# Two elementwise steps of a mixture-of-experts combine moved from VectorE to GpSimd, with other buffer counts

## The chip, the cores and the metric

The kernel runs on one core of a Trainium2 chip. The core has five instruction queues that run side by side and meet through semaphores: TensorE (PE in the profile; its weight loads are PEld), VectorE (DVE), ScalarE (ACT), GpSimd (POOL) and SyncE (SP, which here only starts transfers). Every queue works in the order of its program: an instruction that waits holds back all that stand behind it on its engine. The metric is the device time of one execution in microseconds (us).

## The reference

One transformer block over x of shape (4, 2048, 256), with shifts, scales and gates that come from a conditioning vector:

```python
h = _layernorm(x, axis=-1) * (1 + ca) + sa
x = x + ga * _L0_attn_ref(h, ...)            # 8 heads, causal, a geometric term in the scores
h = _layernorm(x, axis=-1) * (1 + cb) + sb
x = x + gb * _L0_ffn_ref(h, ...)             # 2 shared experts + 16 routed, 4 for each token

# inside _L0_ffn_ref
probs = jax.nn.softmax(xt @ router_w.T, axis=-1)
topk_p, topk_i = jax.lax.top_k(probs, TOP_K)
act = jax.nn.gelu(up_r, approximate=False) * gate[:, :, None]
routed = jnp.einsum('tre,rhe->th', act, routed_down)
return (shared + routed).reshape(b, s, h)
```

All arrays are 32-bit floats. For the part that is changed this is what counts: a token's result is its row after attention and shared experts, plus gb times the weighted sum of four routed experts' outputs.

## The kernel before

The 8192 tokens are worked on in 16 blocks of 512 (`QB`), each in four tiles of 128 (`P`). A loop over the blocks (line 1440) alternates two stages. In a fill-in stage (`fill_in`) TensorE does projections, the output product, the shared experts and tiles of routed experts, mixed with the searches for the score maxima (ps on TensorE, parts on VectorE). In an attention stage (`sum_steps`) it computes scores (st), the products with the values (av) and the sums of the probabilities (dv); VectorE adds neighbouring probability tiles (p<-p,p) so that some dv products can be left out.

The blocks 0 to 13 send their tokens to experts in five groups of 2 or 3 blocks. For a group, GpSimd scatters the tokens' rows into a DRAM table xg, ordered by expert (`scatter`). `tile_steps` fetches tiles of that table (xr) and the weights of their experts (wt) by SyncE, turns them (px), multiplies (pu, py) and writes the outputs to a table yg. Blocks 14 and 15 run all experts densely at the end (`dense_steps`; the weighting of the experts is act<-pw,act on VectorE and the output products are pd).

`combine_steps` (line 1227) brings a group's outputs back. There are 14 x 4 = 56 tiles. For each tile there are:

- `gather`, four times: GpSimd fetches one expert's rows for the 128 tokens from yg by an indirect transfer into got. With the first, SyncE loads row, the tokens' rows after attention and shared experts, from the DRAM tensor pre.
- `combine`: first the stores that are due are issued on SyncE. Then VectorE adds up the four rows with their weights into acc (named sum in the profile), in one TENSOR_SCALAR and three SCALAR_TENSOR_TENSOR instructions.
- `complete`: acc is multiplied by gbs (the gate gb) and row is added. The store to the output is put on a list and issued by the next tile's `combine`.

The order on every engine is the order in which the Python code issues the instructions (`Pinned`, line 43). What sets it here is `tick` (line 501), called at planned moments. A tick first does the next step of a `combine`/`complete` pair that is due, and then one scatter or one gather. A pair falls due three ticks after the last gather of its tile, so in a steady run the order on the queues is: gather 0, 1 and 2 of tile t+1, where `combine` of tile t comes with gather 2; then `complete` of t; then gather 3 of t+1. A new tile's gathers start only while fewer than two pairs are outstanding. Every gather also waits for the last ScalarE instruction issued before it (`paced`). In fill-in stages inside the loop ticks issue gathers but no pairs; pairs wait for the attention stage. After the loop, pairs are issued in all stages.

got, row and sum come from the pool `work`, which keeps two buffers of each unless told otherwise. A load into a buffer waits until the readers of its earlier content are done; so does a computation that writes into one, and a store counts as a reader until its transfer has ended.

Of the kernel before, what the change touches and what calls it, by code (L numbers as in the profile page):

```python
# [12 lines left out]
F32 = mybir.dt.float32  # L13
AF = mybir.ActivationFunctionType
ALU = mybir.AluOpType
# [4 lines left out]
P = 128  # L20
# [74 lines left out]
def adaln_block_kernel(  # L95
# [13 lines left out]
    nc = Engines(tc)  # L109
    B, T, C = x.shape  # L110
# [9 lines left out]
    NB = T // QB  # L120
# [17 lines left out]
    of = out.flatten_outer_dims()  # L138
# [6 lines left out]
    work = ctx.enter_context(tc.tile_pool(name="work", bufs=2))  # L145
# [53 lines left out]
    for k in range(KC):  # L199
# [11 lines left out]
        out=kmask,  # L211
        in_=kmask,
# [43 lines left out]
    for pc in pieces:  # L256
# [6 lines left out]
        out=earlier,  # L263
        in_=earlier,
# [57 lines left out]
    gbs = const.tile([P, B, C], F32, tag="gbs", name="gbs")  # L322
# [173 lines left out]
    stores = []  # L496

    def paced(made):
        nc.gpsimd.behind(made, nc.scalar.last, mybir.DependencyClass.Sync)
# [60 lines left out]
    with tc.tile_pool(name="setup", bufs=1) as setup:  # L560
        wm = setup.tile([P, KC, 6 * C], F32, tag="wm", name="wm")
        nc.scalar.dma_start(
            out=wm[:, :, : 2 * C], in_=wmod[:, : 2 * C].rearrange("(k p) n -> p k n", p=P)
        )
        nc.scalar.dma_start(
            out=wm[:, :, 2 * C :], in_=wmod[:, 2 * C :].rearrange("(k p) n -> p k n", p=P)
# [660 lines left out]
    def combine_steps(group):  # L1227

        n = group.n

        def gather(j, t, k, held):
            i = group.blocks[j]
            at = i * QB + t * P
            if k == 0:
                held["got"] = work.tile([P, TOPK, C], F32, tag="got", name=f"got{i}_{t}")
                held["row"] = work.tile([P, C], F32, tag="row", name=f"row{i}_{t}")
                nc.sync.dma_start(out=held["row"], in_=pre[at : at + P])
            paced(
                nc.gpsimd.indirect_dma_start(
                    out=held["got"][:, k, :],  # L1240
                    out_offset=None,
                    in_=yg[n % 2][: group.nt * P],
                    in_offset=bass.IndirectOffsetOnAxis(
                        ap=group.at[:, j * TT + t, k : k + 1], axis=0
                    ),
                )
            )

        def combine(j, t, held):
            i = group.blocks[j]  # L1250
            got = held["got"]
            while stores:
                stores.pop(0)()
            acc = work.tile([P, C], F32, tag="sum", name=f"sum{i}_{t}")
            held["acc"] = acc
            weight = group.weight[:, j * TT + t]
            nc.vector.tensor_scalar(acc, got[:, 0, :], weight[:, 0:1], None, ALU.mult)
            for k in range(1, TOPK):
                nc.vector.scalar_tensor_tensor(
                    acc, got[:, k, :], weight[:, k : k + 1], acc, ALU.mult, ALU.add  # L1260
                )

        def complete(j, t, held):
            i = group.blocks[j]
            at = i * QB + t * P
            acc, row = held["acc"], held["row"]
            nc.vector.tensor_tensor(acc, acc, gbs[:, i // NB, :], ALU.mult)
            nc.vector.tensor_tensor(acc, acc, row, ALU.add)
            stores.append(lambda: nc.sync.dma_start(out=of[at : at + P], in_=acc))

        out = []
        for j in range(len(group.blocks)):
            for t in range(TT):
                held = {}
                out.append(
                    (
                        [partial(gather, j, t, k, held) for k in range(TOPK)],
                        [partial(combine, j, t, held), partial(complete, j, t, held)],
                    )
                )  # L1280
        return out
# [158 lines left out]
    for i in range(NBLK):  # L1440
# [4 lines left out]
        if i:  # L1445
# [21 lines left out]
            at = max(6, len(mid) - len(finals))  # L1467
# [41 lines left out]
        for n, (_, ss, turn) in enumerate(rest):  # L1509
            at = int(0.93 * (n + 0.5) / len(rest) * ks)  # L1510
# [93 lines left out]
    for e in range(0, R, 4):  # L1604
        nc.sync.dma_start(
            out=resident[:, e * 2 * C : (e + 4) * 2 * C].rearrange("p (e n) -> p e n", e=4),
            in_=experts[e : e + 4].rearrange("e p n -> p e n"),
# [10 lines left out]
    i, j = DENSE  # L1618
# [75 lines left out]
```

## Time and profile before

| | |
|---|---|
| median of 3 runs | 2449.56 us (2446.26 to 2451.17) |
| the profiled execution's own time | 2462.32 us |
| its span, first to last instruction | 2460.6 us |
| mean granted TensorE clock | 0.971 |
| sum<-got,weight on VectorE (56) | 347 ns median |
| sum<-got,weight,sum on VectorE (168) | 485 ns median |
| got<-yg,at on GpSimd (224) | 949 ns median |
| VectorE's waits for a landing of out<-sum | 31.5 us, 8 times, longest 8.4 |
| SyncE's waits put down to VectorE's sum | 308.6 us, 34 times, longest 61.3 |

A name such as sum<-got,weight is a group of instructions that write the tile sum and read got and weight. In groups the columns are shape, count, busy us and mean ns of one, and idle us of the engine just before, with what ended it. In timelines they are start, duration, engine, line, operation, names, shapes and count, and in brackets the idle time before with its releaser. Most instructions pass through one helper, so their line is L54 and the names tell them apart. The profiled execution took 12.8 us longer than the median run.

### The profile page before, as it was taken

The page shows a single profiled execution, that of the slowest core. Times are in us where ns is not written, and L with a number is a line of the kernel's source. Part 1 is how long each engine was busy: PE and PEld are TensorE (multiplying, and loading weights), DVE is VectorE, ACT ScalarE, POOL GpSimd, SP SyncE. Part 2 cuts the span into 40 slices and gives each one's busy share as a digit, 9 for nine tenths or more (in the row PEclk, how much of TensorE's full clock was granted, in tenths as well). Part 3 has the DMA queues.
Part 4 walks back from the last instruction along what each step waited for, and adds up shares of the span by engine and source line. Part 5 has one row for each costly group of instructions (what it writes and reads, how often), then busy time and mean ns, then how long its engine had stood idle before and what let it go on. Part 6 is the DMA issues. An engine that isn't in the chain of part 4 may idle for free.

```text
span 2460.6 us, 42133 instructions
## 1 busy us (share of the span) xinstructions
PE 2318.8 (94%) x16625; PEld 1150.2 (47%) x16625; DVE 1439.9 (59%) x2789; ACT 981.6 (40%) x1391; POOL 732.5 (30%) x740
## 2 busy tenths in 40 slices
PE   7999999999999999999999998998899998998998
PEld 4443434345554334354645435354555634436765
DVE  5676664536674775646674656857564675634325
ACT  2223243543334334533343344643344345552421
POOL 3201010331101244601013342511344125466325
PEclk9889999999999999998999999999999999999999
DMA  3200401343440223323533326222654754427964
GB/s 122 91 1 10 154 10 49 117 162 129 127 155 10 65 65 97 100 86 109 181 120 127 116 63 200 68 89 95 210 188 160 256 161 122 146 72 271 361 202 122
DMA packets 219702, 306.88 MB, mean 125 GB/s; under 512 B 18544, under 2 KB 158832, under 8 KB 219504
## 3 DMA queue, kind: packets, MB, share of 16 engines
q1 hardware_dynamic: 192720, 228.89, 28.5%
q0 software_dynamic: 25536, 73.43, 9.2%
q8 instruction: 131, 2.15, 0.4%
q10 hardware_dynamic: 1248, 1.86, 0.2%
q14 instruction: 67, 0.55, 0.1%
HBM read 193.49 MB, written 114.82 MB: 125 GB/s over the span
## 4 chain that ended last, share of the span: by engine, by line
PE 83%; DVE 6%; ACT 3%; issue 3%; DMA 2%; POOL 1%; another core or an unknown queue 1%; SPq 0%; ACTq 0%; DVEq 0%; POOLq 0%
PE st L54 17%; PE ps L54 13%; PE av L54 11%; PE dv L54 8%; PE pu L54 8%; PE py L54 6%; DVE parts L54 3%; PE pv L54 3%; PE ppq L54 2%; PE px L54 2%; PE po L54 2%; PE pd_s L54 2%; PE pd L54 2%; PE ppk L54 2%; PE pl L54 1%
## 5 line engine op out<-in xcount | busy, mean ns | idle before, releaser
L54 DVE TENSOR_REDUCE parts<-ps 128x2 f32<-128x1024 f32 (+3 forms) x640 | 662.6, 1063 | 323.9 <-PE ps L54 309.7
L54 ACT ACTIVATE p<-st 128x1024 f32<-128x1024 f32 (+3 forms) x640 | 539.3, 894 | 522.9 <-PE st L54 424.2
L54 PE MATMUL st<-qT,kv 32*128 32x512 f32 (+3 forms) x2560 | 404.2, 579 | 16.2 <-ACT p L54 9.8
L54 PE MATMUL ps<-kv,qT 32*128 32x512 f32 (+3 forms) x2560 | 381.9, 602 | 15.6 <-DVE parts L54 10.3
L54 POOL DMA_INDIRECT got<-yg,at x224 | 228.4, 1020 | 332.1 <-ACT p L54 97.6
L54 PE MATMUL av<-p,kv 128*32 128x512 f32 (+3 forms) x2560 | 307.1, 547 | 4.3 <-ACT p L54 3.1
L74 POOL DMA_INDIRECT xg<-rows,at x219 | 219.6, 1003 | 254.0 <-ACT p L54 93.9
L54 PEld LDWEIGHTS st<-qT,kv 32*128 32x128 f32 x2560 | 143.6, 184 | 269.8 <-issue 144.2
L54 PE MATMUL dv<-p,ones 128*32 128x512 f32 (+3 forms) x2224 | 254.0, 527 | 2.2 <-issue 1.9
L54 DVE TENSOR_TENSOR ps<-ps,cmask 128x256 f32<-128x256 f32 x256 | 109.3, 427 | 215.9 <-PE ps L54 184.7
L54 PEld LDWEIGHTS ps<-kv,qT 32*128 32x128 f32 x2560 | 124.2, 190 | 194.1 <-issue 95.2
L54 POOL TENSOR_TENSOR x<-x,tmps 128x512 f32<-128x512 f32 x28 | 35.4, 1265 | 481.3 <-DVE tmps L54 481.2
L54 PE MATMUL py<-wt,tact 128*128 128x256 f32 x608 | 162.2, 401 | 4.7 <-ACT xt L54 2.2
L54 PE MATMUL st<-mT,unit 3*128 3x512 bf16 (+3 forms) x1280 | 165.0, 347 | 0.0
L54 PEld LDWEIGHTS pu<-xt,wt 128*128 128x128 f32 x1216 | 147.6, 194 | 36.5 <-issue 19.8
L54 PE MATMUL pu<-xt,wt 128*128 128x128 f32 x1216 | 158.6, 282 | 3.6 <-DMA wt<-experts 2.5
L54 ACT COPY y<-py 128x512 f32<-128x512 f32 x152 | 89.1, 586 | 164.0 <-PE py L54 160.6
L54 PEld LDWEIGHTS py<-wt,tact 128*128 128x128 f32 x608 | 110.0, 194 | 58.6 <-ACT xt L54 15.0
L54 DVE TENSOR_TENSOR p<-p,p 128x1024 f32<-128x1024 f32 x84 | 106.4, 1307 | 37.9 <-PE av L54 36.8
L54 PEld LDWEIGHTS dv<-p,ones 128*32 128x32 f32 x2224 | 63.3, 110 | 137.4 <-issue 125.7
L54 ACT COPY xt<-px 128x512 f32<-128x512 f32 x152 | 86.6, 587 | 91.4 <-PE px L54 88.8
L54 POOL TENSOR_TENSOR xnb<-xnb,gm 128x256 f32<-128x256 f32 x128 | 106.6, 840 | 47.7 <-issue 19.7
(290 smaller groups left out, 2416.4 us busy)
## 6 DMA issues: line engine op xcount, KB each, us to landing
wt<-experts SPq DMA_DIRECT2D x304, 256.0 KB
xr<-xg SPq DMA_DIRECT2D x76, 512.0 KB
yg<-y SPq DMA_DIRECT2D x76, 512.0 KB
xg<-zeros SPq DMA_DIRECT2D x16, 1024.0 KB
xin<-in_x SPq DMA_DIRECT2D x16, 512.0 KB
x<-in_x SPq DMA_DIRECT2D x16, 512.0 KB
h2d<-xnb POOLq DMA_DIRECT2D x14, 512.0 KB
pre<-x POOLq DMA_DIRECT2D x14, 512.0 KB
```

The costliest lines, as they stand in the source:

```text
L54: made = call(*args, **kwargs)
L74: made = call()
```

## The change

The two instructions of `complete` are issued on GpSimd in place of VectorE. The second one writes its result into row instead of acc, and the output is stored from row. row gets three buffers in place of two and sum one in place of two, so the memory taken is the same.

```diff
-                held["row"] = work.tile([P, C], F32, tag="row", name=f"row{i}_{t}")
+                held["row"] = work.tile([P, C], F32, bufs=3, tag="row", name=f"row{i}_{t}")
...
-            acc = work.tile([P, C], F32, tag="sum", name=f"sum{i}_{t}")
+            acc = work.tile([P, C], F32, bufs=1, tag="sum", name=f"sum{i}_{t}")
...
             acc, row = held["acc"], held["row"]
-            nc.vector.tensor_tensor(acc, acc, gbs[:, i // NB, :], ALU.mult)
-            nc.vector.tensor_tensor(acc, acc, row, ALU.add)
-            stores.append(lambda: nc.sync.dma_start(out=of[at : at + P], in_=acc))
+            nc.gpsimd.tensor_tensor(acc, acc, gbs[:, i // NB, :], ALU.mult)
+            nc.gpsimd.tensor_tensor(row, row, acc, ALU.add)
+            stores.append(lambda: nc.sync.dma_start(out=of[at : at + P], in_=row))
```

## The prediction

> **What bounds the kernel now.** I read the page's busy shares and its chain first, to see which engine sets the end:
>
> ```profile
> span 2460.6 us, 42133 instructions
> ...
> PE 2318.8 (94%) x16625; PEld 1150.2 (47%) x16625; DVE 1439.9 (59%) x2789; ACT 981.6 (40%) x1391; POOL 732.5 (30%) x740
> ...
> PE 83%; DVE 6%; ACT 3%; issue 3%; DMA 2%; POOL 1%; another core or an unknown queue 1%; SPq 0%; ACTq 0%; DVEq 0%; POOLq 0%
> ```
>
> TensorE is the bound nearly everywhere. A saving on VectorE counts only where TensorE stood still for it. So the question is which of the 56 combined tiles sit at such a spot, and what GpSimd's queue does with the steps it gets. Second, the groups by shape, VectorE then GpSimd, for the two steps that move and for the nearest row on their new engine (the same shape, two SBUF operands):
>
> ```profile
> L54 DVE TENSOR_TENSOR sum<-sum,row 128x256 f32<-128x256 f32 x56 | 26.5, 473 | 1.9
> L54 DVE TENSOR_TENSOR sum<-sum,gbs 128x256 f32<-128x256 f32 x56 | 25.2, 450 | 0.9
> ```
>
> ```profile
> L54 POOL TENSOR_TENSOR xnb<-xnb,gm 128x256 f32<-128x256 f32 x128 | 106.6, 840 | 47.7 <-issue 19.7 <-DVE xnb L54 16.9 <-PE st L54 5.5
> ```
>
> Third, the views by tile, for the spread (min/median/max in ns):
>
> ```profile
> L54 POOL TENSOR_TENSOR xnb<-xnb,gm x128: 721/736/1763, 215.4 to 2256.2; 128x256 f32<-128x256 f32 x128
> ```
>
> ```profile
> L54 DVE TENSOR_TENSOR p<-p,p x84: 1206/1219/2185, 478.9 to 2194.3; 128x1024 f32<-128x1024 f32 x84
> ```
>
> Fourth, timelines around every place where the chain passes through "sum" or where TensorE idles near one. Three matter. SyncE, with TensorE behind it, at 1477 us:
>
> ```profile
> 1477.12 0.32 SPq L54 DMA_DIRECT2D row<-pre  x1
> 1477.78 0.34 SPq L54 DMA_DIRECT2D out<-sum  x1
> 1478.43 1.07 SPq L54 DMA_DIRECT2D xr<-xg  x2
> ```
>
> ```profile
> 1484.57 1.09 PE L54 MATMUL px<-ident,xr 128*128 128x128 f32 x4 [3.40 <-DMA xr<-xg]
> ```
>
> VectorE and TensorE at 2000 us:
>
> ```profile
> 1995.67 0.42 DVE L54 TENSOR_TENSOR sum<-sum,row 128x256 f32<-128x256 f32 x1
> 2000.45 0.35 DVE L54 TENSOR_SCALAR sum<-got,weight 128x256 f32<-128x256 f32 x1 [4.36 <-DMA out<-sum]
> ```
>
> ```profile
> 2003.56 3.05 PE L54 MATMUL dv<-p,ones 128*32 128x512 f32 x16 [0.43 <-issue]
> ```
>
> GpSimd and VectorE at the end:
>
> ```profile
> 2375.80 0.95 POOL L54 DMA_INDIRECT got<-yg,at  x1 [33.03 <-DMA row<-pre]
> ...
> 2446.59 0.95 POOL L54 DMA_INDIRECT got<-yg,at  x1 [0.30 <-issue]
> 2449.19 0.95 POOL L54 DMA_INDIRECT got<-yg,at  x1 [1.65 <-ACT act L54]
> ```
>
> ```profile
> 2453.98 1.53 DVE L54 SCALAR_TENSOR_TENSOR sum<-got,weight,sum 128x256 f32<-128x256 f32 x3
> ...
> 2457.21 0.42 DVE L54 TENSOR_TENSOR sum<-sum,row 128x256 f32<-128x256 f32 x1
> ```
>
> Here the last group's 48 gathers run from 2375.8 to the end, about 1.25 us each, and the last tile is stored at 2457.7, 2.9 us before the span ends.
>
> **The change, part by part.**
>
> *Removed from VectorE.* 56 x (0.450 + 0.473) = 51.7 us, 3.6% of its busy time. Most hides behind TensorE, which in the attention stages works on scores, values and sums without a gap; if that cover were gone it would all come back. The 56 stores and row loads stay on SyncE, 128 KB each, so no traffic is added. On the chain stand the steps at 843 (0.48 us) and 881 us (0.85); TensorE idles 1.19 us before the attention scores (st) at 844 and 1.39 at 882, so both come back whole: **-1.3 us**.
>
> *Row buffers, two to three, and the store's source.* Today the load of row t+2 waits in SyncE's queue for the completing step of tile t on VectorE, which is late when VectorE has other work queued. At 1477 us the step at 1476.67 releases the row load, then the store, then xr; xr lands six us later and TensorE loses 3.40 us. After the change that row load waits only for the store of tile t-1 (issued at 1462.04), and the store of tile t for GpSimd. The four additions of that tile end at 1467.4, GpSimd stands free between gathers at 1469.3 and 1471.2, so the steps end near 1471 and xr goes out near 1472 instead of 1478.4. **-3.4 us.** Bounds: 0, if another wait holds xr, and 3.4; I take the upper, since xr directly follows the store there. Elsewhere the store gets later: at 1035.85 GpSimd would reach the steps at 1037.6 and end at 1039.2, 3.4 us later than now, and the xr and weight loads behind it slip. The first transpose they feed comes after the projections that begin at 1057, so it costs 0 while that cover stands, and up to 3.4 without it.
>
> *Sum buffers, two to one.* The first step of tile t+1 now waits for GpSimd's addition of tile t instead of for the landing of the store of t-1 (VectorE idled 31.5 us, eight times, for such landings). In program order the steps of tile t stand ahead of the last gather of tile t+1 on GpSimd, and VectorE waits for that gather anyway, so the new wait hides in it. At 2000 us the old wait cost 4.36 us, the joins of probabilities behind it came late, and TensorE's dv pair took 0.43 + 3.05 instead of the 1.90 of other such pairs. GpSimd is idle there (18 us before 1999.45), so the steps end near 1996. **-1.5 us**, bounds -1.6 and 0. Most of the other seven lie where loads of weights set the pace: 0.
>
> *Added on GpSimd.* 112 x 0.84 = 94 us (at the minimum 81, at the maximum 197); busy 30% to 34%. Queued behind: the last gather of the next tile each time, norms' powers, xnb. Two dense places:
> - 2039 to 2072 us, where GpSimd works 27.9 of 33 us. Four pairs at 1.5 us come before the gather at 2067.43, but less collision shortens neighbouring steps; the gather at 2050.30 slips about 1 us, with it a join and the dv at 2056.30. **+0.8 us** (0 to 3).
> - A norm's power behind a pair, as at 1028.88: VectorE waits 0.95 us already, and would wait 1.4 more less the 0.9 it no longer works. A handful of such cases, mostly covered: **+0.7 us** (0 to 3).
>
> *The last 86 us.* Every tile now costs GpSimd four gathers, 5.0 us, plus a pair, about 1.55 us at the median less 0.15 of shorter gap. Its idle time there is about 17 us beyond the 0.3 gaps; 11 pairs ahead of the last gather take 15.4, plus 2 to 4 us of waiting for VectorE's additions at 2385 and 2392. Walking the queue, the last gather starts near 2452.9 instead of 2449.2. Its rows land 2.1 us later, so the last addition ends at 2455.5, exactly as now; GpSimd finishes at 2457.1 and the store goes out 0.4 us earlier than at 2457.66, the dense block's half 0.2 later. At 2385 VectorE loses two steps on the chain (-0.8), but a late gather delays one expert weighting by 2 us against 1.7 us of room (+0.3) and the last dense half by 0.8. Net **0 us**; bounds -1.2 (all gains, no lag) and +22 (every step at the 1.76 maximum: 11 pairs, each 2.0 us more).
>
> [...] First the row: the joins of probabilities (two SBUF operands) have a mean of 1307 ns in the groups against a median of 1219, so all overlaps with GpSimd cost them 84 x 0.088 = 7.4 us; the weighted additions (mean 521, median 485, 168 of them) another 6.0. Spread over the existing GpSimd work this is about 0.1 us for each of its steps, so 112 new ones give back some 11 of the 51.7 us. [...]
>
> **Sum.** -1.3 - 3.4 - 1.5 + 0.8 + 0.7 + 0 = -4.7 us: against the profiled execution's own 2462.3 us (span 2460.6 and 1.7 around it) 2457.6; that execution was 12.8 us over the median of 2449.56, so in runs **2444.9 us**. Measurement tells apart about 0.2%, 4.9 us; this forecast lies on that edge.
>
> **Rivals.**
> *Slower: GpSimd bounds the last 86 us.* For: its idle time there lies in pieces of 1.2 to 3 us, and my walk uses all of it up. [...] Each 0.1 us more per pair moves the last gather 1.1 us, and the end with it. To end 4.9 us over before it must eat 9.6 us: pairs of some 2.4 us, steps of 1.2, which the rows show only in collisions. At steps of 1.4: 11 x 1.25 = 13.8 us more, 2459.
> *No gain arrives.* xr at 1477 is held by another wait, and the joins at 2000 by ScalarE. Then -1.3 + 1.5 = 0: 2449.8. For: TensorE's idle time in the whole trace is 142 us and rarely names VectorE.
> *GpSimd's queue holds VectorE.* Where GpSimd waits for ScalarE (up to 18.1 us) ahead of a completing step, the single sum buffer stops VectorE and then TensorE. Against: the order above. One 5 us stop in each of five groups: 2470.
> *More gain.* VectorE's relief shortens score maxima everywhere; a sixth of the 41 us left: 2438.
>
> **How the numbers follow.** As worked out 0.60, GpSimd-bound end 0.18, no gain 0.14, held VectorE 0.04, more gain 0.04. The first, taken as 2440 to 2450, splits 0.36 faster, 0.23 same, 0.01 slower; no gain 0.02, 0.10, 0.02; the bound end 0.02 same, 0.16 slower; the last two one way each. Faster 0.42, same 0.35, slower 0.23. Range 2439 to 2459: below lies most of the last case and a tail of the first; above, the bound end with steps over 1.4 us, and the held queue.
>
> **What would show it.** Right: px after xr near 1478 without its 3.4 us; no VectorE wait on landings of out; GpSimd busy near 827 us; steps of 0.73 to 0.85; the last gather 3 to 4 us after its place. Wrong: steps over 1.1 us at the end, TensorE's pd waiting for act there, VectorE waiting for GpSimd's row, or SyncE's stores waiting for GpSimd with px or pu idle behind.

## The result: 0.23% slower, and the profile after

Over twenty runs each the changed kernel takes 2449.4 us (median; 2443.5 to 2457.3), the kernel before 2444.3 us (2437.1 to 2453.0). The ratio is 1.0023, with a 95% interval of 1.0014 to 1.0033: about 5.6 us slower (5.1 by the two medians), where the forecast's likeliest case was 4.7 us faster.

The page of the changed kernel, the same three lines as were read before (span, busy time of each engine, shares of the chain that ended last):

```profile
span 2446.8 us, 42159 instructions
...
PE 2316.0 (95%) x16625; PEld 1149.8 (47%) x16625; DVE 1403.0 (57%) x2677; ACT 980.6 (40%) x1391; POOL 816.8 (33%) x852
...
PE 81%; DVE 6%; POOL 4%; ACT 3%; issue 3%; DMA 3%; SPq 0%; POOLq 0%; ACTq 0%; DVEq 0%
```

What the change set out to move has moved: VectorE (DVE) is 37 us less busy, GpSimd (POOL) 84 us more. But GpSimd's share of the chain went from 1% to 4%. The span is shorter than the 2460.6 us of the profile that the prediction read, and yet the kernel is slower: that earlier execution had stops of its own, as the first experiment below shows. A second profile of the unchanged kernel is therefore the base of comparison from here on.

The moved steps themselves, in the changed kernel's view by tile (least, median and greatest duration in ns):

```profile
L54 POOL TENSOR_TENSOR sum<-sum,gbs x56: 714/736/1361, 844.4 to 2441.7; 128x256 f32<-128x256 f32 x56
L54 POOL TENSOR_TENSOR row<-row,sum x56: 721/724/1661, 845.2 to 2442.5; 128x256 f32<-128x256 f32 x56
```

They cost what the nearest row had said, 0.72 to 0.74 us. The chain of cause lies elsewhere, in the waits. First the second profile of the kernel before, then the changed kernel (who waits <- for what: total us, times, longest; PE is TensorE):

```profile
DVE sum L54 <- DMA out<-sum: 37.0, 8, 8.9
DVE sum L54 <- DMA got<-yg,at: 24.2, 25, 3.7
...
PE px L54 <- DMA xr<-xg: 6.9, 2, 3.5
...
PE px L54 <- DVE rd L54: 2.3, 1, 2.3
```

```profile
DVE sum L54 <- DMA got<-yg,at: 57.9, 36, 3.3
...
DVE sum L54 <- POOL row L54: 40.1, 18, 5.1
...
PE px L54 <- DVE rd L54: 3.3, 1, 3.3
...
PE pd L54 <- DVE act L54: 2.9, 2, 2.5
...
PE dv L54 <- DVE p L54: 2.4, 1, 2.4
```

VectorE no longer waits for stores to land (37.0 us gone), but waits 40.1 us for GpSimd's additions and 33.7 us more for gathered rows. Three of these waits get through to TensorE: dv waits for joined probabilities (p), px stands behind a transposed denominator (rd), and pd waits for a weighted expert (act). Two of the three were not there before.

Where they come from is seen best in the third group of blocks, at 2030 to 2060 us. GpSimd in the changed kernel (start, duration, engine, operation, out<-in, size, idle time before it and what ended that):

```profile
2039.97 2.54 POOL L54 TENSOR_TENSOR xnb<-xnb,gm 128x256 f32<-128x256 f32 x2
...
2043.98 1.01 POOL L54 DMA_INDIRECT got<-yg,at  x1 [0.30 <-issue]
2045.01 0.73 POOL L54 TENSOR_TENSOR sum<-sum,gbs 128x256 f32<-128x256 f32 x1
2045.82 0.72 POOL L54 TENSOR_TENSOR row<-row,sum 128x256 f32<-128x256 f32 x1
2046.69 1.10 POOL L54 DMA_INDIRECT got<-yg,at  x1
```

VectorE in the same stretch:

```profile
2034.36 0.35 DVE L54 TENSOR_SCALAR sum<-got,weight 128x256 f32<-128x256 f32 x1 [3.71 <-POOL row L54]
...
2037.51 0.48 DVE L54 SCALAR_TENSOR_TENSOR sum<-got,weight,sum 128x256 f32<-128x256 f32 x1 [0.88 <-DMA got<-yg,at]
2037.91 5.68 DVE L54 TENSOR_TENSOR p<-p,p 128x1024 f32<-128x1024 f32 x4
...
2056.20 0.48 DVE L54 SCALAR_TENSOR_TENSOR sum<-got,weight,sum 128x256 f32<-128x256 f32 x1 [1.66 <-DMA got<-yg,at]
2056.60 0.71 DVE L54 STREAM_TRANSPOSE rd<-dv 128x512 f32<-128x512 f32 x1
```

And TensorE:

```profile
2039.19 3.06 PE L54 MATMUL dv<-p,ones 128*32 128x512 f32 x8 [2.37 <-DVE p L54]
...
2057.37 1.12 PE L54 MATMUL px<-ident,xr 128*128 128x128 f32 x4 [3.31 <-DVE rd L54]
```

GpSimd has hardly a gap here. Norm products (xnb), gathers and the two new steps follow each other, so everything behind the new steps comes later. VectorE stands 3.71 us ahead of one tile's additions; the joins begin only when these end, at 2037.91; and dv begins at 2039.19 after a stop of 2.37 us, where the second profile of before has none. The second stop is the same chain with rd in place of the joins.

### The profile page after: what moved, and what is told of

It is laid out like the page before. It is cut to its first block, busy times and chain, and to the rows that moved or that the text cites. A ratio compares the mean times of both kernels' runs of the same rounds, so it can differ in the third digit from the quotient of the medians.

```text
span 2446.8 us, 42159 instructions
## 1 busy us (share of the span) xinstructions
PE 2316.0 (95%) x16625; PEld 1149.8 (47%) x16625; DVE 1403.0 (57%) x2677; ACT 980.6 (40%) x1391; POOL 816.8 (33%) x852
## 4 chain that ended last, share of the span: by engine, by line
PE 81%; DVE 6%; POOL 4%; ACT 3%; issue 3%; DMA 3%; SPq 0%; POOLq 0%; ACTq 0%; DVEq 0%
PE st L54 17%; PE ps L54 13%; PE av L54 11%; PE dv L54 8%; PE pu L54 6%; PE py L54 6%; DVE parts L54 3%; PE pv L54 3%; PE po L54 2%; PE ppq L54 2%; PE px L54 2%; POOL got L54 2%; PE pd_s L54 2%; PE ppk L54 2%; POOL xnb L54 1%
## 5 line engine op out<-in xcount | busy, mean ns | idle before, releaser
L54 PE MATMUL st<-qT,kv 32*128 32x512 f32 (+3 forms) x2560 | 403.6, 582 | 13.1 <-ACT p L54 8.3
L54 DVE TENSOR_TENSOR ps<-ps,cmask 128x256 f32<-128x256 f32 x256 | 109.3, 427 | 214.7 <-PE ps L54 184.6
L54 DVE TENSOR_TENSOR p<-p,p 128x1024 f32<-128x1024 f32 x84 | 109.3, 1342 | 46.5 <-PE av L54 46.0
L54 DVE SCALAR_TENSOR_TENSOR sum<-got,weight,sum 128x256 f32<-128x256 f32 x168 | 88.4, 526 | 62.7 <-DMA got<-yg,at 57.9
```

The source lines that it names most:

```text
L54: made = call(*args, **kwargs)
```

## The experiments

Each kernel ran beside the kernel before on the same chip. All experiments but one (e1) and their ratios:

| run | edit, against the changed kernel | ratio to before, 95% |
|---|---|---|
| e2 | both steps on VectorE, buffers as changed | 0.9994 (0.9971 to 1.0017) |
| e11 | the same again | 0.9974 (0.9952 to 0.9996) |
| e3 | GpSimd for the first 34 tiles | 1.0026 (1.0006 to 1.0047) |
| e4 | GpSimd for the last 22 tiles | 1.0021 (0.9999 to 1.0042) |
| e9 | GpSimd for the first two groups (20 tiles) | 0.9974 (0.9954 to 0.9994) |
| e15 | the same again | 0.9947 (0.9925 to 0.9968) |
| e10 | GpSimd for the third group (12 tiles) | 1.0021 (1.0002 to 1.0040) |
| e5 | next gather ahead of the steps | 1.0032 (1.0012 to 1.0053) |
| e6 | addition alone on GpSimd | 1.0046 (1.0023 to 1.0070) |
| e7 | a third step on GpSimd | 1.0128 (1.0097 to 1.0159) |
| e8 | stores one step of a pair later in SyncE's queue | 1.0096 (1.0065 to 1.0127) |
| e12 | the changed kernel again | 1.0018 (1.0002 to 1.0033) |
| e13 | engine alone; buffers and store as before | 0.9988 (0.9969 to 1.0007) |
| e14 | e13 and the gather ahead | 0.9984 (0.9967 to 1.0001) |

These intervals are as wide as the effect. Two finer readings go with them. One is TensorE's stops by place in the program, from the profiles: the idle time of over 0.3 us ahead of its instructions, added up between the same two instructions of each kernel (named by their time in the second profile of before). e2 and e11 are the same kernel; e2's profile has 1.9 us at 2030 to 2075, none at 2385 to 2440, and 108.7 in the whole span, so whole-span sums of single profiles differ by 7 us where the kernel does not.

| stretch, us | before (e1) | buffers only (e11) | first two groups (e9) | third group (e10) | last 22 tiles (e4) | changed | changed (e12) |
|---|---|---|---|---|---|---|---|
| 780 to 900 | 5.3 | 5.3 | 3.2 | 5.3 | 5.3 | 3.2 | 3.2 |
| 900 to 1290 | 13.2 | 13.1 | 12.9 | 13.0 | 13.2 | 12.4 | 13.7 |
| 1460 to 1500 | 4.7 | 2.4 | 0.3 | 3.0 | 2.2 | 0.3 | 0.3 |
| 1975 to 2030 | 3.8 | 2.2 | 2.2 | 3.1 | 2.2 | 3.1 | 2.2 |
| 2030 to 2075 | 2.9 | 1.7 | 1.8 | 6.2 | 1.9 | 6.2 | 6.0 |
| 2385 to 2440 | 0.0 | 0.0 | 0.0 | 0.0 | 3.1 | 2.9 | 2.8 |
| whole span | 107.8 | 101.3 | 99.7 | 113.3 | 107.6 | 107.9 | 109.3 |

The other takes the granted TensorE clock out of the times; it is explained after e1.

### e1: the kernel before, profiled again

The edit: none.

> The kernel of before, profiled a second time. In its first profile TensorE stood still for 3.85 and 1.84 us at 1303 us (releaser unknown), for 7.50 at 2067 (ptb) and for some 6 around 2205, all without a releaser in this kernel's own work. If these are disturbances of that one execution, they are gone here, the span is near 2447, and VectorE's transposes at the end of the stage at 2067 are then covered by nothing. If they belong to the kernel, they come back at the same places and sizes.

Measured: 2439.17 us in one execution, span 2437.5. TensorE's stops of 7.5 us at 2067 and 5.7 us near 1303, which the first profile of before had shown, are not there. The wait of px for xr is there again, 3.42 us:

```profile
1477.72 1.09 PE L54 MATMUL px<-ident,xr 128*128 128x128 f32 x4 [3.42 <-DMA xr<-xg]
```

The span came out 9.5 us under the 2447 us that had been expected, and a stop of 4.62 us before pu near 2204 stands here that the first profile doesn't have. So the prediction read a profile with accidents in it, and one of them (the stop at 2067) covered px, one of the places where the changed kernel loses time.

The executions of the unchanged kernel that recorded their clock, 111 of them, spread from 2428.6 to 2458.8 us, and this spread goes with the mean granted clock of each (the share of TensorE's full clock that was granted, over the span: 0.963 to 0.976; correlation -0.89). A linear fit over 257 executions, with one offset for each kernel, one for each chip and one slope, gives 1.9 us for each 0.001 of the clock and leaves 3.0 us of scatter. The kernels' offsets from the kernel before at equal clock, with 95%:

- the changed kernel (e12) +4.8 (2.0)
- buffers alone (e2, e11) -0.2 and -1.6 (2.0 each)
- first two groups (e9, e15) -5.5 (2.0) and -6.5 (2.5)
- third group (e10) +4.7 (2.0)
- last 22 tiles (e4) +3.1 (2.0)
- first 34 tiles (e3) +1.0 (2.0)
- gather ahead (e5) +6.2 (2.1)
- addition alone (e6) +4.4 (2.3)
- third step (e7) +19.1 (3.3)
- stores later (e8) +13.8 (2.9)
- engine alone, without and with the gather ahead (e13, e14) +2.5 and +2.3 (2.1 each)

A fit like this also takes out what part of the clock a kernel brings about itself; it is read beside the ratios, not instead of them.

### e2 and e11: the buffers and the store, without the engine

```diff
-            nc.gpsimd.tensor_tensor(acc, acc, gbs[:, i // NB, :], ALU.mult)
-            nc.gpsimd.tensor_tensor(row, row, acc, ALU.add)
+            nc.vector.tensor_tensor(acc, acc, gbs[:, i // NB, :], ALU.mult)
+            nc.vector.tensor_tensor(row, row, acc, ALU.add)
```

> The changed kernel with both steps back on VectorE: three row buffers, one sum buffer and the store from row stay. Theory Q (GpSimd's longer queue makes gathers late, VectorE's additions wait for them in order, and TensorE waits for what stands behind them): the whole loss is gone and the gains of the buffers remain, -3.4 us for xr and -1.5 for the joins at 2000, ratio to before about 0.998. Theory B (the new buffer counts or the store from row cost the time): the ratio stays at 1.002.

> The same kernel as in e2 (buffers and store of the change, both steps on VectorE), for a second profile and a tighter interval beside the others: 0.9985 to 1.0005 by theory Q, whose whole loss is GpSimd's; 1.001 to 1.002 if the buffers have a part in the loss.

Measured: 0.9994 and 0.9974, and none of the stops at dv, at px over 1.4 us or at pd. Without the move to GpSimd there is no loss. (Whether the move alone brings it is the question of e13.) At 1475 us the buffers alone leave 2.4 to 3.1 us of the 4.7 us of stops.

### e3 and e4: where the loss is, cut at the end of the main loop

```diff
-            nc.gpsimd.tensor_tensor(acc, acc, gbs[:, i // NB, :], ALU.mult)
-            nc.gpsimd.tensor_tensor(row, row, acc, ALU.add)
+            engine = nc.gpsimd if not state["ended"] else nc.vector
+            engine.tensor_tensor(acc, acc, gbs[:, i // NB, :], ALU.mult)
+            engine.tensor_tensor(row, row, acc, ALU.add)
```

(e4 has the condition the other way round; the flag is set after the main loop, so 34 tiles lie on one side and 22 on the other.)

> The moved steps on GpSimd only while the loop over blocks issues them (34 of 56 tiles), on VectorE after it. Theory Q with both places at fault: TensorE's wait for px of some 3 us and for dv of some 2 us at the end of the attention stage near 2040 to 2055 stay, the last stages run as before; ratio about 1.000 (gains 4.9 and 1.3 against 5.7). If the loss is in the loop alone, the ratio is as with all tiles moved, 1.002.

> The reverse: on GpSimd only after the loop (22 of 56 tiles). Theory Q: TensorE's waits for px and dv near 2050 are gone; the last 86 us keep the wait of 2.5 us for VectorE's weighting (pd) and the gathers 6.55 us apart per tile; ratio about 1.000 (gains 4.9, loss 1.4 to 6 in the stages after the loop). If the end alone is at fault, the ratio is 1.002; if the loop alone, 0.998.

Measured: 1.0026 and 1.0021, each near the whole loss where about 1.000 was expected, so the two ratios tell little. At equal clock the halves add up: less the buffers' -0.9 they cost 1.9 and 4.0 us, and the changed kernel 5.7. The places tell more: e3 keeps the stops at dv (2.35 us) and px (2.93) and has none at pd; e4 has no stop at dv and px (1.33 at most), and keeps the one at the end, in TensorE's timeline:

```profile
2420.70 2.00 PE L54 MATMUL pd<-kv,act 128*128 128x256 f32 x8 [2.70 <-DVE act L54]
```

### e9, e10 and e15: by groups

```diff
-            nc.gpsimd.tensor_tensor(acc, acc, gbs[:, i // NB, :], ALU.mult)
-            nc.gpsimd.tensor_tensor(row, row, acc, ALU.add)
+            engine = nc.gpsimd if n < 2 else nc.vector
+            engine.tensor_tensor(acc, acc, gbs[:, i // NB, :], ALU.mult)
+            engine.tensor_tensor(row, row, acc, ALU.add)
```

(`n == 2` in e10; n is the group's number, from 0.)

> Buffers and store as in the changed kernel, GpSimd does the two steps for the 20 tiles of the first two groups alone (all combined before 1610 us), VectorE for the 36 after them. Theory Q (GpSimd's lengthened queue costs only where it is full, from 2030 us on): none of the stops at 2037 (dv), 2054 (px over 3 us) and 2418 (pd); the gain at 843 to 882 us (about 3 us) and at 1474 us (5 to 7 us, the wait for xr and what follows it) are there in full; ratio 0.997 to 0.999, below the kernel before. [...] Theory K (a stop of TensorE of 2 us or more is followed by 3.4 to 6.8 us at half the granted clock, so that it costs about twice its length): the stretch at half clock that begins at 1476 in the kernel before is gone with the wait for xr; the two near 1374 and 1384, seen so far with GpSimd's steps in the loop, may be there and cost 4 us, and then the ratio is 0.998 to 1.000.

> The opposite half: GpSimd does the two steps for the 12 tiles of the third group alone (combined between 1975 and 2110 us), VectorE for the other 44. Theory Q with K: the stops at dv (2037) and px (2054) come back, each with a stretch at half clock behind it, so 2030 to 2075 us takes 8 to 11 us longer than with both steps on VectorE; the gains at 843 and (in part) 1474 are absent; ratio 1.002 to 1.005. [...]

> The kernel of e9 (GpSimd for the first two groups, VectorE after them) once more: 0.9965 to 0.999, faster than the kernel before, if its 0.9974 was not chance; if it was, 0.999 to 1.001.

Measured: 0.9974 and 0.9947 for the first two groups, 1.0021 for the third. A loss spread evenly over the steps is out: 20 tiles of 56 give a gain, 12 give more than half of the loss. TensorE in e9, at the place of the two stops shown above:

```profile
2041.78 1.04 PE L54 MATMUL dv<-p,ones 128*32 128x512 f32 x8
...
2055.54 0.66 PE L54 MATMUL px<-ident,xr 128*128 128x128 f32 x4 [1.16 <-DVE rd L54]
```

The lag of GpSimd's queue can be read off against TensorE's dv just ahead of this place. That dv and the last gathers of tiles 27 and 28 (counted from 0), in e9:

```profile
2035.87 1.04 PE L54 MATMUL dv<-p,ones 128*32 128x512 f32 x8
```

```profile
2035.36 0.95 POOL L54 DMA_INDIRECT got<-yg,at  x1 [0.31 <-issue]
...
2046.43 0.95 POOL L54 DMA_INDIRECT got<-yg,at  x1 [0.31 <-issue]
```

The same dv and the first of the two gathers in the changed kernel (the second, at 2046.69, is shown above):

```profile
2029.74 2.02 PE L54 MATMUL dv<-p,ones 128*32 128x512 f32 x8
```

```profile
2034.48 1.10 POOL L54 DMA_INDIRECT got<-yg,at  x1 [0.15 <-issue]
```

The gathers start 0.5 us before and 10.6 us after the dv in e9, and 4.7 and 17.0 us after it in the changed kernel: 5.2 and 6.4 us of lag, and the same in e12. The first of them stands ahead of TensorE's first stop, so it is no consequence of it. The lag builds up early: from 2005 to 2060 us no gap on GpSimd is longer than 0.31 us in the changed kernel, and four pairs of steps stand there before the gather at 2034.48.

A share of the stop could also come from VectorE's joins running longer beside GpSimd's steps. The four joins at 2037.91 took 5.68 us; in e9 they run as two pairs of 2.35 us, so that is 1.0 us, against 3.71 and 0.88 us of waiting for GpSimd and for a gather.

The parts add up at equal clock: buffers -0.9, first two groups -5.1 beyond these, third group +5.6, last 22 tiles +4.0, together +3.6 against the +4.8 (2.0) of the changed kernel (runs made twice are averaged; two tiles of the 56, issued in the loop after the third group, are in none of these runs). By both of its ratios e9 is faster than the kernel before, and so than the changed one.

### e7: half as much work again

```diff
+            quarters = row.rearrange("p (a b) -> p a b", b=64)
+            nc.gpsimd.tensor_tensor(
+                quarters, quarters, ones_row.unsqueeze(1).broadcast_to([P, 4, 64]), ALU.mult
+            )
             nc.gpsimd.tensor_tensor(acc, acc, gbs[:, i // NB, :], ALU.mult)
```

> As the changed kernel, with a third step of the same shape on GpSimd for each of the 56 tiles (the fetched row times one, which changes no value), so half as much again of the moved work, some 41 us. Theory Q: the loss grows faster than the work, since the queue is full where it matters: in the last 86 us eleven more steps of 0.74 us, 8.1 us, which end on the path less what slack is left; stops at dv and px between 2030 and 2065 us together 7 to 10 us; ratio 1.005 to 1.009. My forecast's walk of the last 86 us says the same slope (11 times whatever a pair grows by). If the work on GpSimd itself is under cover, and only the order or the buffers cost (theories S and B): 1.002 to 1.004.

Measured: 1.0128, more than expected. From 2385 to 2440 us this kernel takes 12.1 us longer than e1, against 3.3, 3.5 and 4.8 in the changed kernel, e4 and e12: 7 to 9 us more for eleven more steps, the slope of the prediction's walk (8.1). The stops at dv and px are 3.02 and 4.31 us, within the 7 to 10 us together that were expected. TensorE's two stops at the end:

```profile
2409.64 3.44 PE L54 MATMUL pd<-kv,act 128*128 128x256 f32 x8 [3.27 <-DVE act L54]
...
2446.46 0.79 PE L54 MATMUL pd<-kv,act 128*128 128x256 f32 x1 [4.38 <-DVE act L54]
```

So more work on GpSimd is under no cover there.

With this run the stops at 2030 to 2075 us can be set beside the number of steps per tile that GpSimd has in that place: 1.7 to 2.9 us with none (e1, e2, e4, e9, e11, e15), 3.3 with one (e6), 5.9 to 6.8 with two (e3, e5, e8, e10, e12, e13, e14 and the first profile of the changed kernel), 8.5 with three (left out is the first profile of before, with its stop of 7.5 us).

### e5, e13 and e14: the order of GpSimd's queue, or the single sum buffer

e5 issues the next tile's gather ahead of the completing steps instead of behind them. The core of the edit to `tick`:

```diff
-            sums_due[0][1].pop(0)()
+            step = sums_due[0][1].pop(0)
             if not sums_due[0][1]:
                 sums_due.pop(0)
+                late = step
+            else:
+                step()
...
+        if late is not None:
+            late()
```

e13 is the kernel before with two words changed, so that two sum buffers, two row buffers and the store from the sum stay; e14 is e13 with the edit of e5:

```diff
-            nc.vector.tensor_tensor(acc, acc, gbs[:, i // NB, :], ALU.mult)
-            nc.vector.tensor_tensor(acc, acc, row, ALU.add)
+            nc.gpsimd.tensor_tensor(acc, acc, gbs[:, i // NB, :], ALU.mult)
+            nc.gpsimd.tensor_tensor(acc, acc, row, ALU.add)
```

> As the changed kernel, but in the step where GpSimd gets a tile's two completing steps, the gather of the next tile is put ahead of them and not behind. Theory Q (the two steps, and their wait for VectorE's additions, hold up the next tile's last gather, and what stands behind that gather's additions on VectorE comes late): the gather no longer waits for them, so TensorE's stops at dv and px between 2030 and 2065 us, 5 to 6 us together in the changed kernel, fall under 3, the stop of pd near 2430 (2.4 us) falls under 1.5, and the ratio to the kernel before is 0.999 to 1.001. Theory S (SyncE's stores, waiting for GpSimd, hold up loads of weights): the completing steps come later by one gather, the stores too, so it is as slow or slower than the changed kernel, 1.002 to 1.004, and pu's waits for weights grow past 6 us. [...]

> The kernel before with its two completing steps on GpSimd and nothing else: two sum buffers, two row buffers, the result written to the sum and stored from it. Theory Q1 (it is the single sum buffer that holds VectorE: its first addition begins the moment GpSimd's addition of the tile before ends): the waits for GpSimd's addition, 40 us in the changed kernel, are mostly gone, the dv stop near 2037 is under 1 us and px near 2054 under 2.5 us; the landings of stores cost VectorE 30 us or more again; ratio 1.000 to 1.002, since the gain at xr is not there either. Theory Q2 (it is the next tile's last gather, which stands behind the two steps in GpSimd's queue): the stops at dv and px stay at 2 to 3 us and the stop of pd at the end at 2 to 3 us; ratio 1.002 to 1.005.

> As the one before (two sum buffers, two row buffers, both steps on GpSimd), and the next tile's gather put ahead of the two steps. Theory Q1 and Q2 together (each of the two holds VectorE by itself, which is why the gather ahead gained nothing with one sum buffer): here alone both are taken away, dv near 2037 and px near 2054 stop for no more than in the kernel before (under 0.5 and 2.4 us), pd at the end for under 0.5 us; ratio 0.999 to 1.001. If the length of GpSimd's queue alone counts, whatever the order and the buffers: stops and ratio as in e13.

Measured: with the gather ahead (e5) the stop at dv falls to 1.62 us and the one at pd to 1.46, but px's grows to 4.17, so that the two together are 5.8 us where theory Q had asked for under 3, and the time is no better, 1.0032. Theory S had named such a ratio, and pu's waits for weights of over 6 us are there too (6.8); but they are 6.1 and 4.6 us in the two profiles of the changed kernel and 5.0 in e1, so they don't tell the theories apart. VectorE's wait only changed its name:

```profile
DVE sum L54 <- POOL row L54: 89.8, 25, 8.9
...
DVE sum L54 <- DMA got<-yg,at: 11.2, 12, 1.8
```

Without the single buffer (e13) the wait for GpSimd's row is gone, the landings are back, and gathered rows cost the most:

```profile
DVE sum L54 <- DMA got<-yg,at: 67.3, 39, 4.8
...
DVE sum L54 <- DMA out<-sum: 36.8, 9, 9.2
```

while TensorE stops in the same places, no less:

```profile
2033.95 3.06 PE L54 MATMUL dv<-p,ones 128*32 128x512 f32 x8 [2.77 <-DVE p L54]
...
2052.43 1.12 PE L54 MATMUL px<-ident,xr 128*128 128x128 f32 x4 [3.48 <-DVE rd L54]
```

So at the stops theory Q1 (the buffer) falls. The time fits neither theory: 0.9988, where Q1 had asked for 1.000 to 1.002 and Q2 for 1.002 to 1.005. With both taken away (e14) dv stops 1.54 us, px 4.21 and pd 1.74, as in e5. The expectation that the two together would free VectorE was wrong: neither the order nor the buffer, but the length of GpSimd's queue in that place decides the stops, and the order only chooses at which of the three places they are paid.

Left open is why e13 and e14 as wholes come out near the kernel before (0.9988 and 0.9984) with the stops of the changed one. At equal clock they are 2.5 and 2.3 us slower than before, some 2 us better than the changed kernel, about as much as the scatter allows to see; their mean granted clock was 0.971 against 0.969 in the kernel before beside them. By ratios alone e13 lies below the changed kernel: its interval ends at 1.0007, and that of the twenty runs of the result begins at 1.0014 (that of e12 at 1.0002). So it isn't shown that the move alone, with the old buffers, loses time; a part of the changed kernel's loss may need the new buffers besides.

e13 has a second reading: with two row buffers, as before, the 4.7 us of stops at 1460 to 1500 us are down to 0.3. The move of the steps alone was enough to free xr; the third row buffer was not needed for it.

### e6: the addition alone

```diff
-            nc.gpsimd.tensor_tensor(acc, acc, gbs[:, i // NB, :], ALU.mult)
+            nc.vector.tensor_tensor(acc, acc, gbs[:, i // NB, :], ALU.mult)
```

> As the changed kernel, but the multiplication by the gate stays on VectorE and only the addition of the row goes to GpSimd, so half of the moved work. Theory Q: about half of the 7 us that lie between both steps on VectorE (0.9994) and both on GpSimd (1.0023), so 1.0005 to 1.0015; the stops at dv and px between 2030 and 2065 us together 2 to 4 us. Theory S: the store waits for GpSimd as before, only 0.7 us less each, so 1.0015 to 1.0025.

Measured: 1.0046, where 1.0005 to 1.0015 was expected, and no better than with both steps moved (at equal clock +4.4 us against +4.8). The stops at 2030 to 2075 us (3.3) and at the end (0.0) are as small as half the work would have it, but at 1482, where the changed kernel had lost its stop, there is one of 5.15 us. VectorE, then GpSimd, then TensorE there:

```profile
1478.88 0.42 DVE L54 TENSOR_TENSOR sum<-sum,gbs 128x256 f32<-128x256 f32 x1
...
1485.69 0.48 DVE L54 SCALAR_TENSOR_TENSOR sum<-got,weight,sum 128x256 f32<-128x256 f32 x1 [4.15 <-DMA got<-yg,at]
```

```profile
1479.38 0.73 POOL L54 TENSOR_TENSOR row<-row,sum 128x256 f32<-128x256 f32 x1 [7.32 <-DVE sum L54]
```

```profile
1487.31 1.11 PE L54 MATMUL ptb<-ident,xnb 128*128 128x128 f32 x4 [5.15 <-DVE rd L54]
```

The multiplication stands in VectorE's queue behind score maxima; GpSimd's addition waits 7.32 us for it with the next tile's gather behind it; VectorE then waits 4.15 us for that gather with rd behind it. The run was meant as half a dose and is not one: it splits a step between two queues in program order, and each waits for the other.

### e8: the stores later

```diff
-            while stores:
-                stores.pop(0)()
             acc = work.tile([P, C], F32, bufs=1, tag="sum", name=f"sum{i}_{t}")
...
             nc.gpsimd.tensor_tensor(row, row, acc, ALU.add)
+            while stores:
+                stores.pop(0)()
```

> As the changed kernel, but SyncE gets a tile's store only after the next tile's completing steps in program order, so its queue no longer stands waiting for GpSimd's addition. Theory S: SyncE's waits for GpSimd's row fall from 331 us to under 60, pu's waits for weights fall from 6.1 us to near 2.5, and the ratio comes to 0.999 to 1.001. Theory Q: SyncE's waits fall just the same, but the stops at dv and px between 2030 and 2065 us and of pd at the end stay, and the ratio stays at 1.001 to 1.003.

Measured: 1.0096. The edit did not do what it was for: SyncE's wait for GpSimd's additions stays, in the changed kernel and here

```profile
SPq L54 <- POOL row L54: 330.9, 33, 62.3
```

```profile
SPq L54 <- POOL row L54: 309.6, 28, 59.2
```

and its waits for stores to land grow from 79.7 to 103.2 us. Its profiled execution is 12 us faster than the median of its runs, so the trace shows only part of the loss: 16 us more than e1 between 2240 and 2335 us, where weights are loaded. Whether the stores have a part in the changed kernel's loss isn't settled by this run. The stretch 2195 to 2335 gives no sign of it: the changed kernel stands 2.8 us above e1 there in one profile and 2.4 in the other, while the kernels with the new buffers and VectorE in that stretch (e2, e3, e9, e10, e11, e15) lie between 1.4 us below e1 and 6.2 above it.

### e12: the changed kernel again

> The changed kernel itself once more, on the same chip as the three others: 1.001 to 1.0035; in the profile the stops at dv near 2037, px near 2054 and pd near 2418 stand where they stood, each followed by a stretch at half clock (theory K), and none of about 3.4 us for xr near 1478. If these stops move or vanish in a second profile, theory Q rests on one execution's accident.

Measured: 1.0018, with stops of 2.37 us at dv, 3.06 at px and 2.78 at pd in the second profile, and px at 1475 without its wait. The stops are the kernel's, not one execution's. The half clock that theory K expected behind each of them follows all three here; in the first profile it follows dv and px but not pd.

## Why the prediction was wrong

The time itself, 2449.4 us, lies within the forecast's 2439 to 2459 us, but that is luck: the base of three runs from which it was counted, 2449.56, was 5.2 us above the median of twenty. The direction, faster, was wrong. Taken by the forecast's own steps, against e1 and the stretches of the table:

- *VectorE relieved at 843 and 881 us, -1.3.* Right: the stops fell from 5.3 to 3.2 us, 2.1 in place of 1.3.
- *xr at 1477, -3.4.* The stop went, and more: the stretch 1460 to 1500 is 7.0 us shorter, for 4.4 us of stops went, and with them a stretch of 6.8 us at a granted clock of one half, which begins at 1476.4 in e1. Of the two reasons given, earlier steps on GpSimd hold (the store goes out at 1466.44 in place of 1470.90, and xr behind it at 1467.08 in place of 1471.55); the third row buffer was not needed (e13).
- *Joins at 2000, -1.5.* Right in the first profile of the changed kernel, where the stretch 1975 to 2030 is 1.7 us shorter. In the second it is 1.9 us longer, with 10 us at half clock in it; the stops are 3.1 and 2.2 us against 3.8.
- *The new wait on the single sum buffer hides in the wait for the gather.* The wait came with 40.1 us. Taking it away changed no stop (e13), so as a cost it was rightly put at nothing. What failed was the next term, for the gather that it hides in was itself late.
- *The dense place, 2039 to 2072, +0.8 with an upper bound of 3.* This is the step that failed. The stretch 2030 to 2075 takes 8.1 us longer than in e1 (6.7 in e12), and 10.9 longer than in e11, with the same buffers. The working let the gather at 2050.30 slip by about 1 us; that gather, the last of tile 27, came 5.2 us late. It counted pairs from 2039 us on; in the changed kernel the queue had run without a longer gap for some 13 us, with two pairs in it, before it came to that place. It followed the slip to one dv and not to rd, which stands behind the next tile's additions on VectorE; in the profile that it read, the stop of 7.5 us lay ahead of px, and px itself did not wait. And it priced a stop at its own length: against e11 the stops grew by 4.5 us, and the half clock behind them (3.4 and 6.8 us) lost about 5.1 more, together 9.6 of the 10.9 us.
- *Norms' powers, +0.7.* Nothing to be seen: 13.2 us of stops from 900 to 1290 before, 12.4 and 13.7 after.
- *The last 86 us, net 0.* +3.3 and +4.8 us in the two profiles. The idle time of GpSimd there was overrated: beyond the gaps of 0.3 us it was 13.8 us in the profile that the prediction read, not 17, and 11.8 in e1. From its first to its last gather the last group takes 73.4 us in that profile, 71.4 in e1 (and in e2, e3, e9, e10, e11 and e15, too), and 77.6 and 77.8 in the changed kernel, so the last gather came 6.2 and 6.5 us late where 3.7 had been said, and what follows it made up 2.8 and 1.6 us. The place where it would show, the weighting of an expert, was right, but the room there was overrated too. VectorE reaches act only after an addition that waited for a late gather:

```profile
2428.06 0.48 DVE L54 SCALAR_TENSOR_TENSOR sum<-got,weight,sum 128x256 f32<-128x256 f32 x1 [1.69 <-DMA got<-yg,at]
2428.46 1.22 DVE L54 TENSOR_TENSOR act<-pw,act 128x1024 f32<-128x1024 f32 x1
```

```profile
2429.73 1.99 PE L54 MATMUL pd<-kv,act 128*128 128x256 f32 x8 [2.55 <-DVE act L54]
```

  The -0.8 set against it, VectorE's two steps on the chain at 2385, bought no TensorE time: e1 has no stop there to lose (the first profile had one of 1.76 us).
- *What GpSimd's steps give back of VectorE's relief.* VectorE's busy time fell by 33.5 us (1436.5 in e1) where 52.1 us of steps were removed, so 18.6 us came back, against the 11 estimated from the rows; the joins' mean went from 1300 to 1342 ns. In the first profiles of the two kernels the long joins are those beside GpSimd's elementwise steps: 22 joins of the kernel before and 34 of the changed one overlap such a step and took 1.55 and 1.52 us on average, the 62 and 50 others 1.22.

In the first profile the gains, with their clock, came to 12 us (3.4 + 7.0 + 1.7) and the two losses to 11.4 (8.1 + 3.3); the profile stands 9.3 us above e1 in all, and 4.1 of these are half-rate clock at 1374 to 1387 us, which kernels on both sides of the edit show (e9 4.1; e10 and e11 2.9) and others do not (e1, e2, e12). What the kernel loses on average is the fit's 4.8 us. Single profiles do not close this account. Against e11 there are 6.6 and 8.0 us more stops in the two profiles for 6.4 us more time at equal clock; but against e2, the same kernel as e11, the stops are 0.8 us fewer and 0.6 more, and against e1 they are the same (107.8 against 107.9 and 109.3), gains and losses having cancelled. Part of the rest is e1 itself, one execution that lies 1.2 us under the fit at its clock.

So the step that failed is the lateness of GpSimd's queue in its two full places: +0.8 us for the first, where +8.1 and +6.7 were measured, and 0 for the second, where +3.3 and +4.8 were. Of the rivals, the one given 4% came nearest, GpSimd's queue holding VectorE; but not where GpSimd waits for ScalarE, and at the stops not by the buffer: GpSimd is simply full. The rival of a GpSimd-bound end named a right place; the slow steps that it asked for were not needed, for at the end no step took 1.1 us.

## What to carry to other kernels

Before work goes to an engine with idle time, look at where that idle time lies: the same two steps gained some 5 us where GpSimd had gaps and lost 9 to 10 us where it had none (at equal clock, beside the buffers alone), and on average over the span it was idle for two thirds. An engine that issues the gathers delivers whatever its queue does late to all who wait for them, and on an in-order engine the cost falls on what stands behind the waiting instruction (here VectorE's waits of 3.71 and 0.88 us ahead of the joins became TensorE's stop of 2.37 us at dv): follow it further than to the first of them. Take a base profile twice before a stop in it is used as cover, and price a stop of TensorE with the clock that follows it.

## What the runs showed of the hardware that was not expected

In two places of the changed kernel a stop of TensorE cost more than its length. The clock column of the windows view, at the same stretch of the changed kernel and of e9 (length, busy time of each engine with its instructions, then granted clock, DMA share, GB/s):

```profile
2039.40:2042.80 3.40, 3.40 (x12) 0.71 (x12) 3.38 (x3) 1.87 (x2) 3.01 (x3) 0.51 0.18 55
...
2056.40:2063.30 6.90, 5.93 (x14) 3.67 (x15) 2.64 (x6) 1.69 (x3) 2.35 (x3) 0.51 0.26 74
```

```profile
2039.40:2042.80 3.40, 3.40 (x36) 1.08 (x34) 3.37 (x4) 2.66 (x3) 2.88 (x4) 1.00 0.27 77
...
2056.40:2063.30 6.90, 6.90 (x36) 4.98 (x35) 0.88 (x3) 3.26 (x6) 0.95 (x1) 1.00 0.61 187
```

Right behind each of the two stops the granted clock is half, for 3.4 and 6.8 us, and full in e9, which has no stop at dv and one of 1.16 us at px. By estimate, from the clock of 0.51 there, each 3.4 us at half clock is 1.7 us of work lost. Over e1 to e15 and the changed kernel's profile, such a stretch follows the dv stop in all 7 profiles where it lasts 2.3 us or more and in none of the 9 where it lasts 1.7 or less; at px it follows in 10 of the 11 with more than 2.3 us and in none of the 5 with less than 1.6. At pd it is less clear: it follows in 3 of the 6 profiles with 2.5 us or more, and in neither of the 2 with less than 1.8. So in these places no stop under 1.8 us was followed by half clock, and most, but not all, of 2.3 us or more were.

In all 17 profiles of this case every such stretch begins on a grid of 3.4134 us (off it by 0.05 us at most). In the first profiles of the two kernels there are 20 and 23 of them, each 3.41, 6.83, 10.24 or 13.65 us long but for the last, which ends with the trace; the first begins at 49.73 us in the one and at 49.48 in the other. One and the same stop was followed by different lengths: px by 6.8 us at a clock of 0.51 in the changed kernel's first profile and by 3.4 us at 0.50 in its second (e12), pd by none in the first and by half clock in the second. Places with many small stops differ, too: 1372.4 to 1387.4 us went at 0.65 to 0.67 in the changed kernel's first profile, the same place in e1, e2 and e4 at 1.00. Whether it is the place of the grid against the program that decides this, and with it the spread of 30 us between executions of one kernel, which follows the mean granted clock, was not tried.
